# A kernel's late loads, moved from ScalarE's queue to SyncE's and put behind a small store

## The chip, the cores and the metric

The kernel runs on one core of one Trainium2 chip. A core has five engines with an instruction queue each: TensorE (PE, matrix products), VectorE (DVE), ScalarE (ACT), GpSimd (POOL) and SyncE (SP, which here only starts DMA transfers). Each engine takes its instructions strictly in order; an instruction that waits for a semaphore holds up everything behind it on its engine. A DMA transfer is started ("issued") by an instruction on an engine's queue and then runs on the core's 16 DMA engines.

The metric is the device time of one execution in microseconds (us). A second measure, the span, goes from the first to the last instruction in one profiled execution.

## The reference: what is computed

The input x has 4 sequences of 1024 tokens with 256 features. Four residual blocks follow one another, each on a layer norm of x:

```
x = x + LRU(layernorm(x))        # complex linear recurrence over the tokens, then a GELU layer, then a layer norm
x = x + FFN(layernorm(x))        # top-32 gates of two softmaxes, one 256x256 weight
x = x + Attention(layernorm(x))  # 8 heads, keys and values from a 64-wide latent
x = x + FFN(layernorm(x))        # the same weights again
```

The LRU is, per sequence, `h[t] = lam * h[t-1] + gamma * (x W_in)` with complex `lam`, then `out = Re(h) W_mid0 - Im(h) W_mid1 + o`, a two-layer GELU network with a residual, and a layer norm with gain and bias. The FFN has two small grouped convolutions whose batch norm runs over all 4096 tokens, so no FFN result exists before the last token's convolution is done. All weights and biases of the FFN (`w_ffn`, `lin_t`, `rows`) are first needed there; the gain and bias of the LRU's layer norm (`brow`) are needed when the first block of outputs is normalized.

## The kernel before

The tokens are held in SBUF as 32 tiles of 128 tokens by 256 features, in eight blocks of four tiles (`x0` to `x7`; the profile and the text below call the blocks by number). A sequence is two blocks: block 2b holds the even and block 2b+1 the odd tokens of each pair, because the recurrence is done on pairs (`CH = 2`).

The first stage is the LRU. For each block, `head` (L357) takes the layer norm: `bn_stats` and `bn_aggr` on DVE (L133, L134), a chain of small DVE instructions for the inverse root (L55 to L66), ACT applies it (L145), PE transposes (L147), and ACT and DVE split the result in a rounded high half and a rest (`split`, L160 and L161; the tiles are `xnt`). For each sequence and each half `c` of the features, `states` (L381) multiplies by the input weights on PE, ACT evacuates (L390), and DVE multiplies with the cosine and sine tables, scans, and multiplies back (L402 to L416). For each block, `outputs` (L422) makes the output product on PE (into `po`), ACT evacuates it to `ot` (L438), then comes the GELU layer (`pz` L443, `zt` L446), the second layer (`pz` L452), which DVE adds into `ot` (L455), a transposition to `py` (L465), a layer norm on DVE, its application on ACT (`yn`, L474), and on POOL the gain, the bias and the sum into x (L482 to L484). `f1.head` (L501) starts the FFN for a finished block.

Before the first `states`, DVE and ACT build the cosine and sine tables (`ct`, `st`) by doubling (L268 to L275; DVE has the half c = 0, ACT helps with c = 1), and `first_weights` (L277) makes combined input weights: PE transposes them to `pw`, ACT copies the high half to the tile `f` (L160), DVE the rest (L161).

`ffn_weights` (L995) prepares what the FFN needs. POOL clears tiles, DMAs load `lint` (four pieces), `wf`, and then three times a tile `v` of 128 x 256 into which three rows are loaded (L1030). Each `v` is turned to two or three bf16 pieces: ACT copies it (L1031), POOL subtracts (L1032), ACT copies two pieces (L1034), POOL subtracts again (L1035), ACT copies the last (L1036). The pool of `v` has one buffer, so the next rows can only be loaded after the last POOL and ACT instruction on the ones before.

The order of the work on each engine is not written by hand. The program text gives an order of priority, and the scheduler of the framework simulates the program on a time line and issues, on each engine, what it finds ready (`schedule_with_timeline_sim=True`, L1321); any change may move instructions far from the place of the edit. `tc.issue_after(i)` adds one restriction: what is written inside it comes behind instruction `i` on that instruction's engine. Semaphores for DMAs are shared by all queues and used in turn, eight of them, so an issue also waits until the DMA eight places before it has landed.

In the kernel before, x blocks 0 and 1 are loaded by SP at the very start, and everything else in the first stage by ACT: the LRU weights at the start, blocks 2 and 3 after the first split (L1083), `brow` behind the fourth evacuation of a state product (L1088), and blocks 4 to 7 and all loads of `ffn_weights` behind the eighth (`lru.evacuated[7]`, L1095). SP has nothing between the first two loads and the stores of `f1.head` (L527).

Of the kernel before, what the change touches and what calls it, by code (L numbers as in the profile page):

```python
# [10 lines left out]
F32 = mybir.dt.float32  # L11
# [10 lines left out]
P = 128  # L22
B = 4
T = 1024
D = 256
# [3 lines left out]
NBLK = B * T // 512  # L29
# [143 lines left out]
def by_block(v):  # L173

    return [
        v[b * T : (b + 1) * T, :].rearrange("(q p r) d -> r p q d", p=P, r=CH)[r] for b in range(B) for r in range(CH)
    ]
# [807 lines left out]
def run(*gens):  # L985
    for g in gens:
        for _ in g:
            pass
# [6 lines left out]
def ffn_weights(nc, rp, cp, w, lint, lin_t, w_ffn, rows):  # L995
    vecs = w.vecs


    grp = cp.tile([P, 32], F32, tag="grp", name="grp")
    nc.gpsimd.memset(grp, 1.0)  # L1000
    nc.gpsimd.affine_select(
        out=grp, in_=grp, compare_op=ALU.is_ge, fill=0.0, base=0, pattern=[[-4, 32]], channel_multiplier=1
    )
    nc.gpsimd.affine_select(
        out=grp, in_=grp, compare_op=ALU.is_ge, fill=0.0, base=3, pattern=[[4, 32]], channel_multiplier=-1
    )
    for s in range(2):
        for k in range(KD):
            nc.gpsimd.tensor_scalar(
                w.cw[:, k, s * 32 : (s + 1) * 32],  # L1010
                grp,
                vecs[:, V_CW + 2 * s + k : V_CW + 2 * s + k + 1],
                0.0,
                ALU.mult,
                ALU.add,
            )
    nc.gpsimd.memset(lint, 0.0)
    for s in range(2):
        for k in range(KD):
            r = k * 64 + s * 32  # L1020
            nc.scalar.dma_start(lint[r : r + 32, s, :], lin_t[s, k * 32 : (k + 1) * 32, :])
    nc.scalar.dma_start(w.wf, w_ffn)

    nc.gpsimd.memset(w.ones, 1.0)
    parts = [slice(32 * i, 32 * i + 32) for i in range(3)]
    for dst, at in ((w.linb[:, 0:D], 0), (w.linb[:, D : 2 * D], D), (w.bias, 4 * D)):
        v = rp.tile([P, D], F32, tag="v", name="v")
        nc.gpsimd.memset(v, 0.0)
        for i in range(3):
            nc.scalar.dma_start(v[32 * i : 32 * i + 1, :], rows[0:1, at : at + D])  # L1030
        nc.scalar.copy(dst, v)  # L1031
        nc.gpsimd.tensor_tensor(v, v, dst, ALU.subtract)  # L1032
        for i in (1, 2):
            nc.scalar.copy(dst[parts[i], :], v[parts[i], :])  # L1034
        nc.gpsimd.tensor_tensor(v[parts[2], :], v[parts[2], :], dst[parts[2], :], ALU.subtract)  # L1035
        nc.scalar.copy(dst[parts[2], :], v[parts[2], :])  # L1036
# [3 lines left out]
def tile_kernel(ctx: ExitStack, tc: tile.TileContext, x_in, w_lru, vecs_in, rows, w_ffn, lin_t, w_attn, w_down, out):  # L1040
    nc = tc.nc
# [9 lines left out]
    def load_x(engine, blk):  # L1051
        engine.dma_start(blocks[blk], by_block(x_in)[blk])
# [9 lines left out]
    w = Weights()  # L1062
    w.ident, w.vecs = ident, vecs
    w.wf = cp.tile([P, KD, D], F32, tag="wf", name="wf")
    lint = cp.tile([P, 2, D], F32, tag="lint", name="lint")
# [5 lines left out]
    f1 = Ffn("f1", tc, bp, x, w)  # L1071
# [3 lines left out]
    with ExitStack() as c1:  # L1075
        psum = Banks(c1.enter_context(tc.tile_pool(name="ps1", space=PSUM)), {"pu": 2, "po": 2, "py": 2, "pt": 2})

        brow = c1.enter_context(tc.tile_pool(name="brow", bufs=1)).tile([P, 2, D], F32, tag="brow", name="brow")
        lru = Lru(tc, c1, ident, vecs, brow, w_lru, psum)
        xb = [x[4 * k : 4 * k + 4] for k in range(NBLK)]  # L1080
        xnt = [lru.head(xb[0])]
        lru.tables(lambda: xnt.append(lru.head(xb[1])))
        with tc.issue_after(lru.xnt_first):  # L1083
            for blk in range(2, 4):
                load_x(nc.scalar, blk)
        h = [[lru.states(xnt, c) for c in range(KD)]]
        lru.output_weights()
        with tc.issue_after(lru.evacuated[3]):  # L1088
            nc.scalar.dma_start(brow.rearrange("p a b -> p (a b)"), rows[0, 2 * D : 4 * D].partition_broadcast(P))
        xnt += [lru.head(xb[k]) for k in (2, 3)]  # L1090
        h.append([lru.states(xnt[2:4], c) for c in range(KD)])
        for k in range(NBLK):
            last = k >= NBLK - 2
            if k == 0:
                with tc.issue_after(lru.evacuated[7]):  # L1095
                    for blk in range(4, NBLK):
                        load_x(nc.scalar, blk)
                    ffn_weights(
                        nc, c1.enter_context(tc.tile_pool(name="rows", bufs=1)), cp, w, lint, lin_t, w_ffn, rows
                    )  # L1100
            if k < NBLK - 1:
                run(lru.outputs(k % CH, xb[k], xnt[k], h[k // CH], (0, 1), last))

            b = k // CH + 1
            if 2 <= b < B:
                if k % CH == 0:
                    h.append([])
                h[b].append(lru.states(xnt[b * CH : (b + 1) * CH], k % CH))
            if k + 4 < NBLK:
                xnt.append(lru.head(xb[k + 4]))  # L1110
            if 2 <= k < NBLK - 2:
                run(f1.head(k - 2, lru.sp, psum, "pt"))
        for blk in range(4, NBLK - 3):
            run(f1.head(blk, lru.sp, psum, "pt"))
        k = NBLK - 1
        ot, zt = lru.buffers()
        halves = [
            lru.outputs(k % CH, xb[k], xnt[k], h[k // CH], (i,), last, tag, [v[:, :, c : c + 256] for v in (ot, zt)])
            for i, tag, c in ((0, "pu", 0), (1, "po", 256))
        ]  # L1120
        for i in (0, 0, 1):
            next(halves[i])
        run(f1.head(NBLK - 3, lru.sp, psum, "pt"))
        for i in (0, 1, 0, 1, 0, 1, 1):
            next(halves[i])
        with tc.issue_after(lru.last_gelu):
            run(f1.head(NBLK - 2, lru.sp, psum, "pt"))
        run(*(f1.head(NBLK - 1, lru.sp, psum, "pu", (i,), "lx", "zt") for i in range(2)))

    with ExitStack() as c2:  # L1130
# [7 lines left out]
        at = Attention(tc, x, ident, ident64, wqk, wvo, wd, sp, wp)  # L1138
        with ExitStack() as c4:
# [14 lines left out]
            first = at.prepare(0, 0, psum, "at")  # L1154
# [170 lines left out]
```

## Time and profile before

| | |
|---|---|
| device time, median of 3 runs (lowest to highest) | 1529.86 us (1528.63 to 1532.12) |
| device time of the profiled execution | 1528.76 us |
| its span | 1527.0 us |
| busy in the span: PE, DVE, ACT, POOL | 1286.5, 1184.6, 1017.5, 680.3 us |
| mean granted TensorE clock | 0.946 |

The time is 1.76 us more than the span; that part lies around the instructions. Stages, in us from the start of the span, with the busy time of the engines in each:

| stretch | what it is | PE | DVE | ACT | POOL | granted clock |
|---|---|---|---|---|---|---|
| 0 to 38 | first layer norms, tables, first weights | 18.65 | 32.76 | 21.75 | 10.02 | 1.00 |
| 38 to 76 | states of sequences 0 and 1 | 32.48 | 37.65 | 12.24 | 0.00 | 0.96 |
| 76 to 115 | outputs of blocks 0 and 1 | 28.67 | 30.40 | 21.24 | 14.70 | 0.91 |
| 115 to 267 | the other outputs and states, start of the FFN | 142.47 | 98.34 | 57.96 | 49.98 | 0.96 to 1.00 |
| 267 to 300 | end of the first stage | 18.91 | 21.74 | 16.10 | 4.93 | 0.65 |
| 300 to 1260 | first FFN, attention | 859.44 | 736.10 | 727.94 | 446.22 | 0.93 to 0.98 |
| 1260 to 1527 | end of attention, second FFN | 185.92 | 227.62 | 160.30 | 154.45 | 0.86 |

A row is read so: in 38 to 76 DVE works 37.65 of 38 us, so whatever delays DVE there delays what needs it; PE and ACT have slack. In 115 to 267 it is PE that has almost no slack (142.47 of 152). The chain that ended last is, in the last 200 us, mostly DVE (top-k of the second FFN, L674).

### The profile page before, as it was taken

Reading aid. Unit: us, or ns where it says so; the run is one execution under the profiler, and the core shown is the slowest. Engines: PE = TensorE matmul, PEld = TensorE weight load, DVE = VectorE, ACT = ScalarE, POOL = GpSimd, SP = SyncE. Lnnn points to the kernel's source line nnn. Section 1 sums busy time; section 2 is a strip of 40 time slices with the busy share of each in tenths; the row PEclk is TensorE's granted clock in tenths of the full one; section 3 lists DMA queues with packets and bytes.
Section 4 is the critical chain, followed back from the end, with each engine's and each line's share of the span. In section 5 each row is a group of like instructions: output and inputs, shape, how many; then the busy total and the mean of one; then the engine's idle time right before and its main releaser. Section 6 shows DMA issues by size and latency. Waiting matters only on the chain. (4 is left out here: it accounts for less than half of the span.)

```text
span 1527.0 us, 28727 instructions
## 1 busy us (share of the span) xinstructions
PE 1286.5 (84%) x10134; PEld 955.6 (63%) x10136; DVE 1184.6 (78%) x3682; ACT 1017.5 (67%) x2152; POOL 680.3 (45%) x849
## 2 busy tenths in 40 slices
PE   4879998697898898888998989889999999566675
PEld 3535465376677766766776767677777777334454
DVE  8976665697868887878768687777676675599998
ACT  5353433566887877797777787877777776475674
POOL 2033332161545454544544554454344444067776
PEclk9999999698999999999999999999999999688899
DMA  3110000321454343434433445334344545000000
GB/s 118 32 41 15 21 21 21 128 97 49 84 93 90 61 77 73 77 70 82 82 74 60 72 79 86 61 61 83 68 82 79 92 86 96 1 15 24 22 25 28
DMA packets 288609, 96.51 MB, mean 63 GB/s; under 512 B 268233, under 2 KB 284626, under 8 KB 288466
## 3 DMA queue, kind: packets, MB, share of 16 engines
q1 hardware_dynamic: 283024, 88.50, 28.7%
q10 hardware_dynamic: 5442, 6.18, 1.2%
q8 instruction: 80, 1.31, 0.4%
q14 instruction: 63, 0.52, 0.1%
HBM read 16.01 MB, written 11.53 MB: 18 GB/s over the span
## 5 line engine op out<-in xcount | busy, mean ns | idle before, releaser
L898 POOL TENSOR_TENSOR pd<-pr,pd 128x1024 f16<-128x1024 f32 x128 | 273.5, 2141 | 247.6 <-ACT pd L897 185.7
L890 DVE TENSOR_REDUCE nm<-sc 128x1 f32<-128x1024 f32 x256 | 308.5, 1217 | 78.9 <-PE sc L886 77.5
L894 ACT ACTIVATE pr<-sc,nm 128x1024 f32<-128x1024 f32 x256 | 285.9, 1119 | 84.6 <-DVE nm L892 47.0
L886 PE MATMUL sc<-kh,qs 128*128 128x512 f32 x512 | 184.3, 438 | 26.4 <-ACT pr L894 18.8
L886 PE MATMUL sc<-kl,qs 128*128 128x512 f32 x512 | 162.0, 397 | 0.0
L674 DVE MATCH_REPLACE8 wk<-m,wk 128x256 f32<-128x256 f32 x384 | 154.9, 406 | 0.1
L910 ACT COPY p<-ptp 128x512 f32<-128x512 f32 x224 | 124.1, 590 | 45.3 <-PE ptp L905 33.7
L674 DVE MAX8 m<-wk 128x8 f32<-128x256 f32 x384 | 151.3, 412 | 0.4
L930 PE MATMUL pmo<-p,la 128*64 128x128 f32 x2048 | 144.0, 289 | 6.1 <-ACT ft L524 2.9
L905 PE MATMUL ptp<-ident,pr 128*128 128x128 f32 x1024 | 138.3, 275 | 12.9 <-ACT pr L894 12.4
L930 PEld LDWEIGHTS pmo<-p,la 128*64 128x64 f32 x2048 | 122.8, 144 | 25.0 <-ACT ft L524 5.1
L905 PEld LDWEIGHTS ptp<-ident,pr 128*128 128x128 f32 x1024 | 115.6, 140 | 34.8 <-ACT pr L894 22.2
L897 ACT CAST pd<-pr 128x1024 f16<-128x1024 f32 x128 | 133.5, 1054 | 5.6 <-DMA d<-pd 4.6
L886 PEld LDWEIGHTS sc<-kh,qs 128*128 128x128 f32 x512 | 85.2, 195 | 51.1 <-ACT pr L894 29.8
L886 PEld LDWEIGHTS sc<-kl,qs 128*128 128x128 f32 x512 | 97.0, 190 | 23.2 <-issue 1.4
L930 PE MATMUL pmo<-d,lb 128*64 128x128 f16 x3072 | 103.4, 222 | 7.6 <-DVE qs L853 2.6
L930 PEld LDWEIGHTS <-lb 128*64 128x64 f16 x3072 | 92.2, 111 | 26.3 <-issue 20.1
L628 POOL TENSOR_TENSOR ex<-ex,wk 128x512 f32<-128x512 f32 x61 | 77.6, 1273 | 57.4 <-DVE wk L674 45.5
L926 POOL COPY rows<-rs 128x128 f32<-128x128 f32 x128 | 36.1, 294 | 124.4 <-PE pmo L938 76.3
L941 DVE TENSOR_TENSOR on<-pmo,rb 128x128 f32<-128x128 f32 x128 | 36.4, 285 | 66.8 <-ACT rb L940 66.3
L147 PE MATMUL pt<-ident,xn 128*128 128x128 f32 x256 | 47.8, 309 | 44.5 <-ACT xn L145 32.9
L699 PE MATMUL pf<-wf,vt 128*128 128x256 f32 x288 | 81.2, 427 | 4.6 <-ACT vt L697 4.2
(307 smaller groups left out, 2768.6 us busy)
## 6 DMA issues: line engine op xcount, KB each, us to landing
tt<-ft SPq DMA_DIRECT2D x16, 256.0 KB
tt<-tt SPq DMA_DIRECT2D x8, 512.0 KB
out<-x SPq DMA_DIRECT2D x32, 128.0 KB
x<-in_x ACTq DMA_DIRECT2D x6, 512.0 KB
pf<-pfs SPq DMA_DIRECT2D x12, 256.0 KB
full<-pf SPq DMA_DIRECT2D x24, 128.0 KB
d<-pd SPq DMA_TRANSPOSE x128
wa<-in_w_attn SPq DMA_DIRECT2D x2, 640.0 KB
```

Of the source, the lines that this page charges most:

```text
L147: nc.tensor.transpose(pt[:, k, i * P : (i + 1) * P], xn[:, k * P : (k + 1) * P], ident)
L628: pool.tensor_tensor(ex, ex, wk, ALU.subtract)
L674: ins = make(*args).ins
L699: nc.tensor.matmul(dst, vt[:, k, :], w.wf[:, k, :], start=(k == 0 and bias is None), stop=(k == KD - 1))
L886: nc.tensor.matmul(sc[:, sl], qs[:, j, q * P : (q + 1) * P], kk[:, sl], start=(i == 0), stop=(i == 1))
L890: nc.vector.tensor_reduce(nm, sc, AX.X, ALU.max, negate=True)
L894: nc.scalar.activation(pr, sc, AF.Exp, bias=nm, accum_out=ssum[:, j : j + 1])
L897: nc.scalar.copy(pd[:, 0, :], pr)
L898: nc.gpsimd.tensor_tensor(pd[:, 1, :], pr, pd[:, 0, :], ALU.subtract)
L905: nc.tensor.transpose(pt[:, kk, :], pr[:, kc * P : (kc + 1) * P], self.ident)
L910: nc.scalar.copy(dst, pt)
L930: nc.tensor.matmul(po[j * HD : (j + 1) * HD, 0, :], v, pts[j][:, c, :], start=(n == 0), stop=(n == len(terms) - 1),)
```

## The change

All loads that ACT issued late in the first stage are issued by SP instead: the layer norm's rows `brow`, x blocks 4 to 7, the four pieces of `lint`, `wf`, and the nine row loads into `v`, 19 issues in all. They are no longer restricted by evacuations on ACT. In their place SP gets one new DMA, a store of one float per partition (128 x 4 bytes) of the normalized block 1 (`xnt[1][0]`) into a scratch tile `gate` in DRAM, which nobody reads; the store must wait until ACT has written the first half of that tile, and the loads are restricted to come behind it on SP's queue.

```
@@ ffn_weights
-            nc.scalar.dma_start(lint[r : r + 32, s, :], lin_t[s, k * 32 : (k + 1) * 32, :])
-    nc.scalar.dma_start(w.wf, w_ffn)
+            nc.sync.dma_start(lint[r : r + 32, s, :], lin_t[s, k * 32 : (k + 1) * 32, :])
+    nc.sync.dma_start(w.wf, w_ffn)
...
-            nc.scalar.dma_start(v[32 * i : 32 * i + 1, :], rows[0:1, at : at + D])
+            nc.sync.dma_start(v[32 * i : 32 * i + 1, :], rows[0:1, at : at + D])
@@ tile_kernel
         h = [[lru.states(xnt, c) for c in range(KD)]]
         lru.output_weights()
-        with tc.issue_after(lru.evacuated[3]):
-            nc.scalar.dma_start(brow.rearrange("p a b -> p (a b)"), rows[0, 2 * D : 4 * D].partition_broadcast(P))
+
+        gate = f1.dram.tile([P, 1], F32, tag="gate", name="gate")
+        first = nc.sync.dma_start(gate, xnt[1][0][:, 0, 0:1].bitcast(F32)).ins
+        with tc.issue_after(first):
+            nc.sync.dma_start(brow.rearrange("p a b -> p (a b)"), rows[0, 2 * D : 4 * D].partition_broadcast(P))
+            for blk in range(4, NBLK):
+                load_x(nc.sync, blk)
         xnt += [lru.head(xb[k]) for k in (2, 3)]
         h.append([lru.states(xnt[2:4], c) for c in range(KD)])
         for k in range(NBLK):
             last = k >= NBLK - 2
             if k == 0:
-                with tc.issue_after(lru.evacuated[7]):
-                    for blk in range(4, NBLK):
-                        load_x(nc.scalar, blk)
+                with tc.issue_after(first):
                     ffn_weights(
                         nc, c1.enter_context(tc.tile_pool(name="rows", bufs=1)), cp, w, lint, lin_t, w_ffn, rows
                     )
```

Line numbers in the text are those of the kernel before; behind L1092 the changed kernel's are up to three higher.

## The prediction

> **What bounds the kernel now.** I read the page first: PE is busy 84% and DVE 78% of the span, and the chain that ended last is mostly DVE in the second FFN, far from the edit. The edit lies in the first stage, which everything after it waits for, so I read that stage next: the windows, then the time lines of ACT, PE and DVE.
>
> The time line of ACT around the loads (start, duration, engine, line; in brackets the idle time before):
>
> ```profile
> 72.19 0.78 ACT L390 ACTIVATE u<-pu,gb,par_o 128x512 f32<-128x512 f32 x1 [2.02 <-DVE h L402]
> 72.20 2.05 ACTq L1052 DMA_DIRECT2D x<-in_x  x4
> 74.29 2.02 ACTq L1021 DMA_DIRECT2D lint<-in_lin_t  x4
> 76.35 0.43 ACTq L1022 DMA_DIRECT2D wf<-in_w_ffn  x1
> 77.16 4.96 ACTq L1030 DMA_DIRECT2D v<-in_rows  x3
> 82.17 1.26 ACT L438 ACTIVATE ot<-po,ob 128x512 f32<-128x512 f32 x2 [9.20 <-DMA wf<-in_w_ffn]
> 83.33 0.40 ACT L1031 CAST linb<-v 128x256 bf16<-128x256 f32 x1
> ```
>
> Issuing holds ACT's queue from 72.20 to 82.12, because each `v` load waits for the x block eight issues before it. `ot` of block 0 waits 9.20 us for that. On PE the wait is this:
>
> ```profile
> 72.00 2.74 PE L437 MATMUL po<-h,wm 128*128 128x512 f32 x6
> 82.91 5.17 PE L443 MATMUL pz<-ot,w_lru 128*128 128x512 f32 x8 [8.18 <-ACT ot L438]
> ```
>
> PE is idle 8.18 us and then at half clock (5.17 us for what takes 3.60 later). That looks like the gain. But DVE:
>
> ```profile
> 36.00:60.00 24.00, 19.75 (x93) 15.62 (x92) 24.00 (x46) 10.69 (x21) 0.00 (x0) 0.93 0.04 12
> 60.00:91.00 31.00, 20.75 (x60) 11.60 (x59) 30.50 (x89) 8.50 (x15) 1.93 (x3) 0.89 0.25 81
> ...
> 93.10 0.75 DVE L455 SCALAR_TENSOR_TENSOR ot<-pz,vecs,ot 128x512 f32<-128x512 f32 x1 [2.21 <-issue]
> ...
> 115.89 0.74 DVE L455 SCALAR_TENSOR_TENSOR ot<-pz,vecs,ot 128x512 f32<-128x512 f32 x1
> ```
>
> The third busy column is DVE: 24.00 of 24, then 30.50 of 31. It never idles from 5.05 to 90.9, right through PE's gap, and then waits only 2.21 us for the first addition (L455, block 0). So of the 8 to 9 us that ACT and PE lose, DVE could use about 2.
>
> **The change part by part.** I use the scheduled order of the changed kernel on each engine, with the durations of the profiled execution of before (1528.76 us; 1.1 below the median, so I add the sum to the median).
>
> *Removed from ACT:* 19 issues (1 + 4 + 4 + 1 + 9). *Added to SP:* the store and these 19. Nothing is behind them on SP until the stores of L527 at 134.38, so SP's waits cost nothing. ACT's saving is taken up in the DVE sum below.
>
> *When the loads now land.* The store waits for ACT's first copy of block 1's `xnt` (19.56 + 0.58), so it goes at 20.2. The store itself is not in the trace; the nearest rows, other issues, take 0.23 to 0.53, I take 0.4. `brow` took 0.35, so block 4 is issued at 20.95. Before, the first x issue to the third `v` issue took 81.9 - 72.2 = 9.7 us, limited by the data (365 GB/s at best); `brow`'s 256 KB ahead of it adds 0.7. So the third `v` load goes at 31.3 and lands by 32.75: before it went at 81.9 and ACT's copy ran at 83.33, at most 1.4 later. The bounds: 31.3 (no `brow` delay, landing at once: 30.65 + 0.7) and 35 (twice the landing time and a store that holds the shared semaphores 1 us). I take 32.75, from the same loads' own row.
>
> *The wait that moves with the loads.* In the new order ACT's `linb<-v` (L1031) stands just ahead of these copies:
>
> ```profile
> 29.00 0.58 ACT L160 CAST f<-pw 128x512 fp32r<-128x512 f32 x1 [0.28 <-PE pw L290]
> ...
> 30.54 0.67 DVE L161 TENSOR_TENSOR f<-pw,f 128x512 fp32r<-128x512 f32 x1
> ```
>
> ACT stands at L1031 until 32.75, so `f` is copied from 33.1 to 33.7 instead of 29.0. Behind it on ACT are the weight copies and ACT's share of the tables; DVE waits for both. DVE arrives at its `f` instruction at 30.54 + 1.4 (four statistics of block 4 now ahead of it, 0.35 each) + 0.3 (block 4 lands at about 25.2, DVE asks at 24.9) = 32.25 and waits 1.4; the second `f` costs 0.4 (two weight copies between, 1.87 us on ACT against 1.5 on DVE); two copies L1034 (0.81) stand ahead of table steps that DVE wants at once, 0.8; and the second round's L1034, which wait for POOL (0.67 to 0.94 a subtraction), 0.6. The second and third `v` loads (2.8 us from ACT's last copy to landing) are covered by 3.3 and 4.7 us of other ACT work.
>
> *POOL against DVE.* Six POOL subtractions move from 83 to 99, where DVE partly idles, to 33 to 52, where it does not. Small DVE instructions beside POOL work took 0.65 us instead of 0.15 (109.7 to 113.8). Each of five more such meetings costs between 0 and 0.5; I take 1.5 of at most 2.5, since DVE is in small table steps for half of them.
>
> *DVE's sum.* Ahead of the first L455 the new order has two more splits (0.6 each), five more small steps (0.1) and one product less (0.6): 90.9 + 1.1 = 92.0. With x4 0.3, `f` 1.4 + 0.4, 0.8, 0.6 and POOL 1.5, which are 5.0, DVE reaches it at 97.0, 3.9 later than the 93.10 of before. PE and ACT will have been ready since about 85: their gain ends in a wait for DVE.
>
> *From there to the second L455.* Before: 22.8 us, because DVE crept through block 6's small steps beside POOL. In the new order those steps come earlier, and PE's chain sets the time: `py` starts 1.0 after L455, two output products with their transposes 11.0, GELU layer and evacuations 4.4, the second layer's half 2.9: 19.3, and 0.8 to the next `py`. PE, however, is idle some 9 us before it and will start at half clock; the 82.91 row prices that: 5.17 - 3.60 = 1.6. So `py` of block 1 starts at 97.0 + 19.3 + 0.8 + 1.6 = 118.7; before it started at 116.68. Then it was PE that was cold (2.91 instead of 1.64 for six products at 117.02), which falls away: -1.3. First stage: 118.7 - 116.7 - 1.3 = +0.7. From there to 267 PE is busy 94% and the order is nearly the same, so the shift passes to the end.
>
> *The tail.* The attention stage keeps its order but for a few neighbours. At the very end before does the last tile's `xg` first:
>
> ```profile
> 1520.87 0.73 DVE L658 TENSOR_TENSOR xg<-xg,ex 128x256 f32<-128x256 f32 x1
> 1521.53 0.41 DVE L651 TENSOR_TENSOR ob<-ob,ex 128x256 f32<-128x256 f32 x1
> 1521.86 0.41 DVE L662 TENSOR_TENSOR x<-x,pf 128x256 f32<-128x256 f32 x1
> ```
>
> The new order is x (L662 of the tile before, which waits for PE until about 1521.75), `ob`, `xg`. The product that ends the kernel needs `xg`, which then ends at 1522.9 instead of 1521.6: +1.3 (between 0.4, if the tile before is ready a step earlier, and 1.3).
>
> Sum: +0.7 + 1.3 = +2.0; 1529.86 + 2.0 = 1531.9, with 0.2% (3.1 us) about what a measurement can tell from no change.
>
> **What the skill says.** The Trainium skill, "DMA: Bandwidth & Descriptors", rules for kernel authors, advises issuing a DMA early and waiting on its semaphore late, so that the fixed cost is overlapped. The change issues early, but the row of L1031 shows the wait moving early too; by the rule's happy case the 1.8 us at `f` would vanish and the sum be +0.2, by the rows it is +2.0.
>
> **The rivals.**
>
> *The gap's length passes through (faster).* If the `v` rows land before ACT asks and POOL meets DVE at no cost, DVE reaches L455 at 92.0 + 0.3: 4.7 earlier than in my sum, so -2.7 in all; with PE warm (-1.6) and the tail free (-1.3) -5.6, about 1524. For it: the 9.20 and 8.18 us in the rows. Against: DVE's 30.50 of 31. It decides where the third `v` load lands before 31.3.
>
> *The early wait grows (slower).* If `v` lands at 35, DVE waits 2.3 longer; if ACT then also stands for the second and third round (one 1.4 us landing each) and POOL costs its full 2.5, DVE is 6.1 later than in my sum: +8, 1538. It decides where ACT stands at L1031 past 34.
>
> *The loads were hidden anyway.* DVE stays the bound and stalls cancel the 2.2 us that it idled: the first stage is unchanged, the tail varies by 1, 1530 to 1531.
>
> *It does not do what it says.* Ruled out for the issues (the new order has none on ACT), open only for how early they run.
>
> **How the numbers follow.** My forecast 0.40: +2.0, own range -1 to +5.5 (the unknown costs above); of it 0.20 within 0.2%, 0.17 slower, 0.03 faster. The growing wait 0.25, all slower. The passing gap 0.22, all faster. Hidden anyway 0.13, of it 0.11 within, 0.01 slower, 0.01 faster. Together faster 0.26, same 0.31, slower 0.43. The range leaves out about 0.1 at each side: from the passing gap's 1524 to the growing wait's 1538.
>
> **What would show it.** In the changed kernel: no issue on ACT past 17, SP issuing from 20.2 to about 46; ACT idle ahead of `linb<-v` until about 32.7; `f` copied near 33; DVE idle a few us between 30 and 46 and then none until the first L455, near 97; PE idle some 9 us before it; the second L455 near 117.5; `xg` last on DVE but one. It is wrong if ACT does not wait at the first L1031, if DVE reaches the first L455 before 93, or if the stages behind 300 change their length by more than 2 us.

## The result and the profile after

| | before | changed |
|---|---|---|
| median of 6 runs each (lowest to highest) | 1529.24 us (1526.09 to 1532.12) | 1541.09 us (1538.48 to 1547.19) |
| ratio, 95% interval | | 1.0078 [1.0055, 1.0101] |
| device time of the profiled execution; its span | 1528.76; 1527.0 | 1541.56; 1539.8 |
| mean granted clock | 0.946 | 0.933 |

The changed kernel is slower by 0.78%, 11.9 us. The forecast was 1531.9, with a range to 1538.0: the sign was the likeliest one, the size is outside the range.

The time line of the changed kernel: SP's issues first, then DVE and ACT at the tables, and the first L455 (start, duration, engine and line; in brackets the idle time before and what ended it).

```profile
20.32 0.34 SPq L1090 DMA_DIRECT2D gate<-xnt  x1
20.71 0.42 SPq L1092 DMA_DIRECT2D brow<-in_rows  x1
21.19 10.05 SPq L1052 DMA_DIRECT2D x<-in_x  x4
36.31 17.43 SPq L1030 DMA_DIRECT2D v<-in_rows  x9
...
34.84 1.08 DVE L133 BATCH_NORM_STATS2 lx_st<-x 128x6 f32<-128x256 f32 x3 [9.84 <-DMA x<-in_x]
...
36.81 0.51 ACT L354 ACTIVATE turned<-wt,lam 128x256 f32<-128x256 f32 x1 [11.68 <-DVE tw L355]
40.75 0.41 ACT L1031 CAST linb<-v 128x256 bf16<-128x256 f32 x1 [0.80 <-issue]
41.06 0.58 ACT L160 CAST f<-pw 128x512 fp32r<-128x512 f32 x1
...
102.19 1.42 DVE L455 SCALAR_TENSOR_TENSOR ot<-pz,vecs,ot 128x512 f32<-128x512 f32 x2
```

DVE stops for 9.84 us, for data of x block 4, a block that it read first at 75.75, without a wait, in the kernel before:

```profile
75.75 1.08 DVE L133 BATCH_NORM_STATS2 lx_st<-x 128x6 f32<-128x256 f32 x3
```

In the changed kernel ACT then waits 11.68 us for DVE, and `f`, which the prediction put at 33, is copied at 41.06. The wait that the prediction was about, ACT's at the first `linb` copy, is 0.80 us. The two additions of the first L455 come at 102.19 instead of 93.10.

What the DMA engines did in that stretch, by windows of 4 us (length; busy time and count of PE, PEld, DVE, ACT, POOL; granted clock; share of DMA time; GB/s):

```profile
20.00:24.00 4.00, 2.06 (x5) 0.79 (x4) 4.00 (x21) 2.48 (x7) 0.35 (x2) 1.00 0.05 7
24.00:28.00 4.00, 3.79 (x9) 3.02 (x10) 1.01 (x10) 1.07 (x4) 1.00 (x6) 1.00 0.12 9
28.00:32.00 4.00, 0.84 (x2) 0.12 (x1) 0.00 (x0) 0.00 (x0) 0.00 (x0) 1.00 0.65 67
32.00:36.00 4.00, 0.00 (x0) 0.00 (x0) 1.16 (x6) 0.00 (x0) 0.00 (x0) 0.57 1.05 351
```

From 20 to 28 only 7 and 9 GB/s are moved, though the issues of `brow` and of blocks 4 and 5, 1.25 MB, are done at 22.17. The trace's landing events point at the store: it is issued at 20.32, and its 16 landing events stand between 24.07 and 28.34. `brow`, issued at 20.71, has landed at 33.26; in the kernel before it took from 45.99 to 49.26. Block 4, issued at 21.19, has landed at 34.75.

The loss does not all arise there. The table compares the same instruction in the two profiled executions: the first L455, the first L674 (the start of the first FFN's top-k, at 299.99 before), an L890 of the attention (at 451.6 before), and the span.

| | first L455 | start of top-k | in the attention | span |
|---|---|---|---|---|
| changed, later by | 9.1 us | 4.7 us | 11.4 us | 12.8 us |

Of 9.1 us the first stage gives back 4.4. Then the stretch from 300 to 451, which the prediction left unchanged, adds 6.7, and the rest 1.4. The place in the first FFN is seen on ACT and PE. Before:

```profile
345.30 3.64 ACT L587 ACTIVATE xc_f<-xc_f,bt,bs 128x512 f32<-128x512 f32 x5
348.84 0.45 ACT L650 ACTIVATE ob<-pf,rs 128x256 f32<-128x256 f32 x1
349.19 0.80 ACT L587 ACTIVATE xc_f<-xc_f,bt,bs 128x512 f32<-128x512 f32 x1
...
349.34 1.99 PE L567 MATMUL pfa<-wf,tt 128*128 128x256 f32 x8 [2.04 <-ACT ob L650]
```

Changed:

```profile
352.24 4.35 ACT L587 ACTIVATE xc_f<-xc_f,bt,bs 128x512 f32<-128x512 f32 x6
356.59 1.28 ACT L155 ACT_TABLE_LOAD   x1
358.00 0.46 ACT L650 ACTIVATE ob<-pf,rs 128x256 f32<-128x256 f32 x1
...
358.50 3.78 PE L567 MATMUL pfa<-wf,tt 128*128 128x256 f32 x8 [3.98 <-ACT ob L650]
```

The scheduler, which plans the whole program anew, has put `ob` of the sixth tile behind the sixth GELU and the table load, instead of ahead of the sixth. PE waits 3.98 us for it instead of 2.04, and then does eight products in 3.78 us instead of 1.99 (the granted clock is 0.50 from 356.9 to 363.6). Together that is 3.7 us (1.94 + 1.79).

### The profile page after: what moved, and what is told of

It is laid out like the page before. It is cut to its first block, busy times and chain, and to the rows that moved or that the text cites. A ratio compares the mean times of both kernels' runs of the same rounds, so it can differ in the third digit from the quotient of the medians.

```text
span 1539.8 us, 28733 instructions
## 1 busy us (share of the span) xinstructions
PE 1302.1 (85%) x10134; PEld 964.6 (63%) x10136; DVE 1180.7 (77%) x3682; ACT 1019.2 (66%) x2152; POOL 682.7 (44%) x849
## 5 line engine op out<-in xcount | busy, mean ns | idle before, releaser
L890 DVE TENSOR_REDUCE nm<-sc 128x1 f32<-128x1024 f32 x256 | 309.1, 1219 | 82.8 <-PE sc L886 81.2
L674 DVE MATCH_REPLACE8 wk<-m,wk 128x256 f32<-128x256 f32 x384 | 170.8, 459 | 0.1
L674 DVE MAX8 m<-wk 128x8 f32<-128x256 f32 x384 | 167.0, 463 | 0.4
L905 PE MATMUL ptp<-ident,pr 128*128 128x128 f32 x1024 | 138.7, 275 | 12.5 <-ACT pr L894 11.8
L699 PE MATMUL pf<-wf,vt 128*128 128x256 f32 x288 | 88.3, 456 | 4.3 <-ACT vt L697 3.9
```

What stands on the lines that cost most here:

```text
L674: ins = make(*args).ins
L699: nc.tensor.matmul(dst, vt[:, k, :], w.wf[:, k, :], start=(k == 0 and bias is None), stop=(k == KD - 1))
L890: nc.vector.tensor_reduce(nm, sc, AX.X, ALU.max, negate=True)
L905: nc.tensor.transpose(pt[:, kk, :], pr[:, kc * P : (kc + 1) * P], self.ident)
```

## The experiments

Theory S: the store's 128 pieces of 4 bytes are slow to write to DRAM and hold everything behind them on SP's transfers. Rivals: it is `brow`'s broadcast, or the number of pieces, or the early waits of the prediction. Theory O: the loss past 300 comes from the new instruction order; its rival is that it comes from the lateness of the first stage or from the clock.

| kernel | store | median, us | ratio to before, interval | first L455 | top-k start, shift | attention, shift |
|---|---|---|---|---|---|---|
| changed | 128 x 4 B to DRAM | 1541.09 | 1.0078 [1.0055, 1.0101] | 102.2 | +4.7 | +11.4 |
| e1_row_gate | 1 x 512 B to DRAM | 1532.29 | 1.0021 [1.0004, 1.0037] | 94.3 | -3.6 | +0.6 |
| e2_sbuf_gate | 128 x 4 B to SBUF | 1535.29 | 1.0033 [1.0018, 1.0049] | 94.6 | -3.9 | -3.6 |
| e3_brow_last | 128 x 4 B to DRAM | 1539.99 | 1.0077 [1.0047, 1.0108] | 101.7 | +4.8 | +11.4 |
| e4_wide_gate | 128 x 512 B to DRAM | 1534.36 | 1.0034 [1.0021, 1.0048] | 95.0 | +0.3 | +3.8 |
| e5_ob_first | 128 x 4 B to DRAM | 1541.87 | 1.0080 [1.0068, 1.0093] | 103.9 | +9.0 | +11.6 |
| e6_held_casts | 1 x 512 B to DRAM | 1528.49 | 0.9989 [0.9977, 1.0000] | 92.3 | -4.1 | -0.9 |
| e7_x_only | 1 x 512 B to DRAM | 1529.94 | 0.9997 [0.9983, 1.0011] | 91.3 | -6.5 | -5.9 |
| e8_held_ob | 1 x 512 B to DRAM | 1523.78 | 0.9975 [0.9964, 0.9986] | 92.9 | -4.8 | -5.3 |
| e9_early_casts | 1 x 512 B to DRAM | 1532.79 | 1.0033 [1.0016, 1.0050] | 94.0 | -1.5 | +7.0 |

Ratios are to the kernel before on the same chip, so they, not the medians, compare kernels of different rows. The shifts come from one profile each, against the profile before. They spread by some us for reasons of their own: the changed kernel, e3 and e5 have the same order up to 300 and the same store, and start the top-k 4.7, 4.8 and 9.0 us late. The profiles of e2 and e7 were their fastest runs (1526.88 of up to 1537.42, 1525.19 of up to 1533.22), so their late shifts flatter them; that of e9 was its slowest (1538.49, the median is 1532.79).

**The store in one piece (e1).**

```
-        gate = f1.dram.tile([P, 1], F32, tag="gate", name="gate")
-        first = nc.sync.dma_start(gate, xnt[1][0][:, 0, 0:1].bitcast(F32)).ins
+        gate = f1.dram.tile([1, P], F32, tag="gate", name="gate")
+        first = nc.sync.dma_start(gate, xnt[1][0][0:1, 0, 0:P].bitcast(F32)).ins
```

> The store reads 512 bytes of one partition of the same tile and writes them as one piece, instead of 4 bytes of each of 128 partitions; what it waits for is the same. Theory S (the store's 128 four-byte pieces into DRAM hold SP's transfers: in the changed kernel it is issued at 20.32 and its last piece lands at 28.34): brow takes about the 3.3 us that it took before, block 4 lands at 25 to 27 instead of 34.75, DVE's 9.84 us wait for it falls below 1.5, the first L455 comes at 94 to 97 instead of 102.2, and of the 11.9 us lost 3 to 7 come back (1534 to 1538). Theory B (not the store, but the broadcast of one row behind it is slow): block 4 still lands past 30, DVE waits over 5 us, the time stays near 1541. The schedule is drawn anew, so what the first FFN costs may change too; it is read by itself, as the shift between 300 and 450.

The store landed at 21.39, 1.09 us after its issue (a first event of its semaphore stands at 20.73, but its one packet of data starts at 21.03), and `brow` took 4.7 us; block 4 had landed at 26.80. The time line:

```profile
20.30 0.31 SPq L1090 DMA_DIRECT2D gate<-xnt  x1
20.66 0.36 SPq L1092 DMA_DIRECT2D brow<-in_rows  x1
21.07 2.23 SPq L1052 DMA_DIRECT2D x<-in_x  x4
...
26.89 1.08 DVE L133 BATCH_NORM_STATS2 lx_st<-x 128x6 f32<-128x256 f32 x3 [1.24 <-DMA x<-in_x]
```

DVE's wait is 1.24 instead of 9.84, the four x issues take 2.23 instead of 10.05. The kernel gains 0.57% on the changed one (1.0078 to 1.0021), 8.7 us and so a little more than the 3 to 7 expected; its order is drawn anew, so not all of that need be the store's. Past 300 it has no stall at `ob`, but PE waits 5.48 us for a copy (L581). Theory B falls: the broadcast is not what held block 4 past 30. It is not free either: with `brow` ahead of it block 4 took 5.7 to 6.0 us from issue to landing (e1, e2, e4), without it 3.6 to 4.3 (e6 to e9).

**The same pieces into SBUF (e2).**

```
-        gate = f1.dram.tile([P, 1], F32, tag="gate", name="gate")
+        gate = cp.tile([P, 1], F32, tag="gate", name="gate")
```

> The same 128 pieces of 4 bytes, but written to a tile in SBUF instead of DRAM. If it is small writes to DRAM that are slow (S, narrow form): block 4 lands at 25 to 27 and the first stage goes as with the one-piece store. If small pieces are slow wherever they go: the store takes 4 to 8 us again and block 4 lands at 32 to 35. Theory B: block 4 lands past 30 although the store is short. The instruction order on PE, DVE, ACT and POOL is that of the one-piece store.

The store's issue and DVE's wait for block 4:

```profile
20.06 0.55 SPq L1090 DMA_DIRECT2D gate<-xnt  x1
...
27.14 1.08 DVE L133 BATCH_NORM_STATS2 lx_st<-x 128x6 f32<-128x256 f32 x3 [1.39 <-DMA x<-in_x]
```

128 pieces of 4 bytes landed 1.76 us after their issue (20.06 to 21.82) when they went to SBUF, block 4 at 27.04, and DVE waited 1.39. So small pieces are not slow wherever they go: it is DRAM. In time e2 lies at 1.0033 against e1's 1.0021, with the same order on PE, DVE, ACT and POOL; the intervals overlap.

**brow behind the blocks (e3).** The line of `brow` stands behind the loop over blocks 4 to 7; nothing else differs.

> The changed kernel with one difference on SP alone: brow is issued behind the four x blocks instead of ahead of them; the order on all other engines is unchanged. Theory S: the store still holds the queue to 28.3, so block 4 lands at 29 to 31, about 4.5 us earlier, DVE waits 4 to 6 us instead of 9.84, the first L455 comes about 4 us earlier, and 1 to 4 us of the time come back. Theory B: block 4 lands by 26, DVE's wait is gone, and the first stage gains its full 4.7 us. If all of the x4 wait is covered by something else, nothing changes.

DVE's wait, and then four windows of this run:

```profile
33.43 1.08 DVE L133 BATCH_NORM_STATS2 lx_st<-x 128x6 f32<-128x256 f32 x3 [7.76 <-DMA x<-in_x]
```

```profile
21.00:25.00 4.00, 1.90 (x5) 0.78 (x5) 4.00 (x24) 2.20 (x6) 0.35 (x2) 1.00 0.12 17
25.00:29.00 4.00, 4.00 (x10) 2.94 (x10) 0.67 (x6) 0.66 (x3) 0.95 (x6) 1.00 0.79 45
29.00:31.00 2.00, 0.29 (x2) 0.00 (x0) 0.00 (x0) 0.00 (x0) 0.00 (x0) 1.00 0.28 25
31.00:33.00 2.00, 0.00 (x0) 0.00 (x0) 0.00 (x0) 0.00 (x0) 0.00 (x0) 0.85 0.95 319
```

Block 4 landed at 33.34, so 1.4 us earlier, not 4.5 as theory S expected and not 8.7 as theory B did; DVE waited 7.76; time and shifts are those of the changed kernel. Both numbers were wrong, mine because I thought that block 4 stood still until the store had landed (28.95 here) and then ran freely. It did neither. Its packets run from 21 on, but slowly: single ones of 1 KB take up to 5.4 us, against at most 0.6 in the kernel before, and the core moves 17 to 45 GB/s until 31, some 2 us past the store's last landing. Why the slowness outlasts the store I can't say.

**Pieces of 512 bytes, the same order (e4).**

```
-        gate = f1.dram.tile([P, 1], F32, tag="gate", name="gate")
-        first = nc.sync.dma_start(gate, xnt[1][0][:, 0, 0:1].bitcast(F32)).ins
+        gate = f1.dram.tile([P, P], F32, tag="gate", name="gate")
+        first = nc.sync.dma_start(gate, xnt[1][0][:, 0, 0:P].bitcast(F32)).ins
```

> The store writes 512 bytes of each of the 128 partitions (64 KB in 128 pieces) instead of 4 bytes of each; all instructions stand in the same order as in the changed kernel on every engine, SP too. Size theory (pieces of 4 bytes are slow to write to DRAM): the store lands within 2.5 us of its issue, block 4 at 26 to 28, DVE waits under 2.5 us for it, and the end of the first stage is 3 to 4 us ahead of the kernel before instead of 4.7 behind. Count theory (128 pieces are slow whatever their size): the store lands past 24, block 4 past 31, the first stage ends behind the kernel before. For the first FFN: if its loss of 6.7 us (shift +4.7 at 300, +11.4 at 450) comes from the new instruction order, it comes again, and the time is 1530 to 1534; if it came from the lateness of the first stage, it is gone and the time is 1524 to 1527.

64 KB in 128 pieces landed in 1.57 us (20.27 to 21.84), where 512 bytes in 128 pieces had taken 8.0. The time line and two of the windows:

```profile
20.27 0.34 SPq L1090 DMA_DIRECT2D gate<-xnt  x1
21.14 2.20 SPq L1052 DMA_DIRECT2D x<-in_x  x4
...
27.27 1.08 DVE L133 BATCH_NORM_STATS2 lx_st<-x 128x6 f32<-128x256 f32 x3 [1.44 <-DMA x<-in_x]
```

```profile
20.00:24.00 4.00, 2.02 (x5) 0.79 (x4) 3.95 (x19) 1.81 (x5) 0.00 (x0) 1.00 0.45 120
24.00:28.00 4.00, 3.03 (x7) 2.45 (x8) 2.56 (x17) 1.79 (x5) 1.29 (x8) 1.00 0.93 315
```

315 GB/s stand where 9 stood. This is the cleanest price of the store, since every instruction is in the changed kernel's order: 1.0078 to 1.0034, 0.44% or 6.7 us (7.8 by the spans of the two profiles); by the two intervals it is some 3 to 11 us. The count of pieces is ruled out. What is left need not be the size alone: in the changed kernel all 128 pieces fall into one stretch of 512 bytes of DRAM, here each has a stretch of its own, and no run separates the two. The first stage ended +0.3, not the -3 to -4 that I expected here. Past 300 a loss came again, +3.4 us, with the same stall:

```profile
353.79 3.78 PE L567 MATMUL pfa<-wf,tt 128*128 128x256 f32 x8 [3.97 <-ACT ob L650]
```

The stall belongs to the order, not to lateness. The changed kernel lost 3.3 us more there, at a granted clock of 0.90 against 0.94 in e4.

The Trainium skill, "DMA: Bandwidth & Descriptors", Specifications, gives as the least transfer for line rate "≥512 B (below this, SDMA does read-modify-write)". The runs agree: 1.57 us for pieces of 512 bytes, 8.0 for pieces of 4; no run has a size between them. The section "Why small descriptors are slow (HBM only)" of the same page says that "SBUF↔SBUF transfers don't suffer this penalty", and the 1.76 us of e2 agree. That the cause is a read and a write back of each piece no run here shows. The prediction drew on another rule of that page and passed this one over, the one that spoke against the change.

**ob ahead of the last GELU (e5).**

```
-            nc.scalar.mul(ob, pf, rs[:, 0:1])
+            self.last_ob = nc.scalar.mul(ob, pf, rs[:, 0:1]).ins
...
-                            g = f1.gelu(blk)
+                            with tc.issue_after(f1.last_ob if blk == NBLK - 1 else f1.last_exp): g = f1.gelu(blk)
```

> The changed kernel with the original store, and one restriction more: ACT's last GELU of the first FFN (L587) comes behind the evacuation ob (L650) of the sixth tile, where it stood in the kernel before. The first stage is as in the changed kernel (first L455 at 102, shift +4.7 at 300). Theory (order): PE's wait for ob at 358 falls from 3.98 to about 2 us, the eight pfa products behind it run at full clock (2.0 instead of 3.78), the shift at 380 is +6 to +8 instead of +10 to +11, the time 1536 to 1539. Rival (the loss lies in the clock's windows, whatever the order): the shift at 450 stays at +10 or more, the time near 1541.

```profile
356.03 3.63 ACT L587 ACTIVATE xc_f<-xc_f,bt,bs 128x512 f32<-128x512 f32 x5
359.57 0.45 ACT L650 ACTIVATE ob<-pf,rs 128x256 f32<-128x256 f32 x1
...
360.08 1.99 PE L567 MATMUL pfa<-wf,tt 128*128 128x256 f32 x8 [1.76 <-ACT ob L650]
```

The stall did what was expected: 1.76 instead of 3.98, and 1.99 instead of 3.78. From 300 to 451 the kernel lost 2.6 us (+9.0 to +11.6) instead of 6.7. But the time did not move: the shift at 450 and the time are what the rival had forecast, though the shift was +9.0 already at the start. The profile's first stage was 4.3 us longer, by chance as far as the order goes (block 4 landed at 35.95, and DVE waited 10.63 for it), and the attention, whose order the restriction had also redrawn, lost some 2 us more (+13.6 from 1100 on, against +11.5). One stall can be removed by a restriction, but the order of everything behind it is drawn again.

**The rows held (e6), and then ob too (e8).** e6 takes the one-piece store, leaves `brow` with ACT as before, and holds ACT's first copy of each row tile behind the fourth evacuation:

```
+        with tc.issue_after(lru.evacuated[3]):
+            nc.scalar.dma_start(brow.rearrange("p a b -> p (a b)"), rows[0, 2 * D : 4 * D].partition_broadcast(P))
+        gate = f1.dram.tile([1, P], F32, tag="gate", name="gate")
+        first = nc.sync.dma_start(gate, xnt[1][0][0:1, 0, 0:P].bitcast(F32)).ins
         with tc.issue_after(first):
-            nc.sync.dma_start(brow.rearrange("p a b -> p (a b)"), rows[0, 2 * D : 4 * D].partition_broadcast(P))
...
-def ffn_weights(nc, rp, cp, w, lint, lin_t, w_ffn, rows):
+def ffn_weights(tc, hold, nc, rp, cp, w, lint, lin_t, w_ffn, rows):
...
-        nc.scalar.copy(dst, v)
+        with tc.issue_after(hold):
+            nc.scalar.copy(dst, v)
...
-                        nc, c1.enter_context(tc.tile_pool(name="rows", bufs=1)), cp, w, lint, lin_t, w_ffn, rows
+                        tc, lru.evacuated[3], nc, c1.enter_context(tc.tile_pool(name="rows", bufs=1)), cp, w, lint, lin_t, w_ffn, rows
```

> One-piece store; brow stays with ACT as in the kernel before; x4 to x7 and the feed-forward loads by SP behind the store; ACT's first copies of the rows (L1031) come behind the fourth evacuation, so that ACT waits for no row while the tables are built. On PE the first FFN and the attention stand almost in the order of the kernel before. My theory: DVE has no wait for x above 1 us and none for f, the first L455 comes at 91 to 94, the first stage ends 3 to 5 us ahead of the kernel before, and with the old order behind it this stays: 1524 to 1527, faster than both. If a loss past 300 comes with any earlier end of the first stage (not with the order), the shift at 450 is 3 us or more worse than at 300, and the time 1528 to 1533.

The first stage went as expected: no wait of DVE for x or `f`, first L455 at 92.3, top-k 4.1 us earlier. The rest did not. The scheduler again put `ob` behind all six GELUs, PE waited 3.95 us and was slow behind it, and 3.2 us of the gain went: the ratio is 0.9989, with an interval that reaches 1.0000. e8 adds the restriction of e5 to this kernel.

> The kernel with the held row copies and one restriction more: the last GELU of the first FFN behind the evacuation ob (L650) of the sixth tile, as in the kernel before. With it the order from the first FFN on is almost that of the kernel before on all engines. Theory (order): PE's wait for ob at 348 falls from 3.95 to about 2 and the eight products behind it run at full clock, so the 4 us that the first stage gains are kept to the end: shift -3 to -5 at 450, 1525 to 1527, faster than the kernel before by 0.2 to 0.3%. Rival (windows of half clock eat any gain): 1528 to 1530, no difference from the held copies alone.

Here the restriction left the order past 300 almost as in the kernel before. First the kernel with the rows held, then with `ob` ahead as well:

```profile
348.01 3.62 PE L567 MATMUL pfa<-wf,tt 128*128 128x256 f32 x8 [3.95 <-ACT ob L650]
```

```profile
344.38 1.99 PE L567 MATMUL pfa<-wf,tt 128*128 128x256 f32 x8 [1.74 <-ACT ob L650]
```

The gain of the first stage is kept: -4.8 at the top-k, -5.3 in the attention, 0.9975 [0.9964, 0.9986]. This is the fastest kernel of the study, 3.8 us (0.25%) below the kernel before. What the restriction alone is worth stays open: the intervals of e6 and e8 overlap.

**Only the x blocks (e7).** `brow`, `lint`, `wf` and the rows stay with ACT and their old evacuations; x4 to x7 go to SP behind the one-piece store:

```
         with tc.issue_after(first):
             for blk in range(4, NBLK):
                 load_x(nc.sync, blk)
...
                 with tc.issue_after(lru.evacuated[7]):
                     ffn_weights(
```

> Only x4 to x7 move to SP, behind the one-piece store; brow, lint, wf and the rows stay with ACT behind the same evacuations as in the kernel before. If ACT's 9.20 us wait ahead of ot was made by the data of the x blocks (each row load waiting for the block eight issues before), it falls to about 4 us (eight issues of 0.4 to 0.5), PE's idle 8.18 falls alike, and the first L455 comes at 90 to 93. If DVE alone sets the first stage, its end is within 1 us of the kernel before; if PE's gap counted, it is 2 to 4 us ahead. Time 1525 to 1530 with the first FFN's order near the old one.

ACT's issues:

```profile
67.47 1.76 ACTq L1021 DMA_DIRECT2D lint<-in_lin_t  x4
69.27 0.43 ACTq L1022 DMA_DIRECT2D wf<-in_w_ffn  x1
69.74 1.10 ACTq L1030 DMA_DIRECT2D v<-in_rows  x3
```

The data were the cause of ACT's long issue: without the x blocks ahead, ACT issued the eight loads from 67.47 to 70.84 without a wait, and PE's 8.18 us of idle time ahead of `pz` is gone. The first L455 came at 91.3, and the first stage ended 6.5 us earlier in that profile. That is more than the 1 us allowed for if DVE alone set its end; how much of it is PE's gap and how much the redrawn order the run does not tell. In the median nothing is left (0.9997). Past 300 this order has a stall of its own, PE waiting 5.48 us for a copy (L581) that stands behind the GELUs.

**The early copies priced (e9).** e6 without the holding, so that ACT's first `linb` copy stands ahead of `f` again:

```
-        with tc.issue_after(hold):
-            nc.scalar.copy(dst, v)
+        nc.scalar.copy(dst, v)
```

> The kernel with the held row copies, without the holding: ACT's first linb copy stands again right ahead of f (L160), as in the changed kernel; store in one piece, brow with ACT as before. This prices the early wait and POOL's early subtractions: by the prediction's terms (f 1.8, L1034 1.4, POOL 1.5) DVE reaches the first L455 4 to 5 us later than with the copies held (96 to 97 against 92.3) and the first stage ends 3 to 5 us later. If the row loads, landing earlier now that the store is short, cost ACT nothing, the first L455 stays within 1 us of 92.3. Past 300 the order is that of the changed kernel, with PE's 4 us stall at ob: 1530 to 1535.

ACT's first `linb` copy and what DVE waited for behind it:

```profile
31.20 0.41 ACT L1031 CAST linb<-v 128x256 bf16<-128x256 f32 x1 [1.45 <-DMA v<-in_rows]
...
32.05 0.58 DVE L355 SCALAR_TENSOR_TENSOR wm<-w_lru,lam,turned 128x256 f32<-128x256 f32 x1 [0.76 <-ACT turned L354]
```

First L455 at 94.0 against 92.3 with the copies held: the early copies cost DVE 1.7 us, not 4 to 5. ACT waited 1.45 us at `linb`, and DVE waited 0.76 us for the weights that ACT turned behind it, then 0.52 and 0.29; with the copies held it had none of these waits, so little is left for POOL. DVE had no wait at `f` above 0.2 us. The first stage ended 2.6 us later than in e6, within the spread of single profiles but on the side expected. Past 300 the 3.96 us stall and a loss of 8.5 us.

**The clock from 300 to 451.** Over all eleven profiles the length of this stretch goes with the TensorE clock granted in it: at 0.95 (before, e2, e7, e8) it takes 151.2 to 152.2 us, at 0.92 to 0.94 (e4, e5, e6) 154.2 to 155.1, at 0.89 to 0.91 (changed, e1, e3, e9) 155.8 to 160.1. In the changed kernel PE is busy 7.1 us longer there than before, for the same number of products. The order does not fix this clock: e1 and e2 have the same order, and were granted 0.91 and 0.95. So one profile can't price the order alone, and what starts the windows of half clock I didn't test.

## Why the prediction was wrong

**The step that failed: the store.** In "When the loads now land" I wrote that the store "itself is not in the trace", took "other issues, 0.23 to 0.53" as the nearest rows, and bounded its hold by 1 us. The issue did take 0.34. But what counted was the landing, and for that no row of an x or weight load is near, since none writes to DRAM or moves pieces of 4 bytes. It took 8.0 us; block 4 was put at 25.2 and came at 34.75, the third row load at 32.75 and came at 40.68. The term "x4 0.3" was 9.84, and "SP's waits cost nothing" was wrong with it. By e4 this is 6.7 of the 11.9 us.

**With the store short, the first stage was nearly as forecast.** In e4, the changed kernel's own order, the third row load landed at 33.16 (forecast 32.75), `f` was copied at 33.54 (33.1), the first L455 came at 95.0 (97.0), 20.4 us lay between it and the second (20.5), and the stage ended at +0.3 (+0.7). Of DVE's 5.0 us of stalls 3.0 came (95.0 less my 92.0). Two terms in it were wrong: DVE did not wait for `f` (1.8 in my sum), and waited 1.44 for x4 instead of 0.3. Block 4 landed at 27.18 and not 25.2, because `brow` ahead of it cost some 2 us and not the 0.7 of my sum (e1). The 20.4 is in part luck. My 1.6 for half clock in it came from PE idling some 9 us ahead of the first L455; PE waited only 1.39 and 1.32 us there, a window of half clock came all the same, from 96.5 to 99.9, and in the changed kernel, with the same order but no such window, the stretch took 18.8.

**The second step that failed: "the shift passes to the end".** I compared the order of the attention and of the tail, and not that of the first FFN's GELUs. e4 puts the loss there at 3.4 us without any lateness. With `ob` put back, PE waits 2.2 us less and its eight products take 1.8 (e5) and 1.6 us (e8) less, and the stretch is 4.1 and 3.7 us shorter. But the granted clock of the whole stretch rose too (0.90 to 0.93, 0.92 to 0.95), and it varies without a change of order, so how much of the 6.7 us is the order alone stays open.

**The tail** was right in sum, not in working. `xg` stands last on DVE but one, but the addition two places ahead of it did not wait: `xg` ended 11.8 us late where the last step of the top-k was 11.6 late, so the order cost 0.2, below my lower bound of 0.4. Another 0.9 came because the last product took 2.07 us instead of 1.13.

**The rivals.** "The gap passes through" describes what the move can be worth without the slow store and the early copies: it priced -5.6 us, and e7 and e8 end the first stage 6.5 and 4.8 us early; e8 keeps it. DVE was the bound up to the first L455, as its 30.50 busy of 31 us said (91.3 and 92.9 against 93.10); the gain came behind it, where 22.8 us to the second L455 became 18.8 and 18.7. "The early wait grows" had the right sign and the wrong wait: it is DVE at block 4 (9.84 us), not ACT at the rows (0.80), and not POOL: DVE's waits alone, 10.3 us, make up what it came later than 92.0.

## What to carry to other kernels

A small store used as a gate is a transfer like any other: price its landing, and not its issue, and give it one piece of 512 bytes rather than 128 of 4 (1.09 us against 8.0 here). What stood behind the slow store on SP's queue was late with it (block 4 landed at 33 to 36 instead of 24 to 27), so such a gate must not stand ahead of data that an in-order engine asks for early; whether loads on another queue would have been spared no run here shows. Where a scheduler plans the program, compare the new order from end to end, and at every place where an engine evacuates for another: one evacuation put behind six GELUs cost PE 3.7 us at that place, and one restriction took that away, though the measured time of the kernel did not clearly follow.

## What the runs showed of the hardware that I had not expected

A store of 512 bytes to DRAM took 8.0 us in 128 pieces of 4 bytes, 1.57 us for 128 times as many bytes in as many pieces, 1.09 us in one piece, and 1.76 us in 128 pieces to SBUF. Transfers behind the slow store ran slowly while it landed and for some 2 us after it (e3: 25 GB/s from 29 to 31, then 319). And DVE's 9.84 us without work at 25 to 35 shrank on the way: between the changed kernel and e4, which share their order, 7.2 us were left at the first L455, 5.5 at the second and 4.4 at the start of the top-k.
